# Feed-forward normalisations on ScalarE with factors by GpSimd; scale and bias of the last feed-forward's second norm on VectorE

## The chip, the cores and the metric

The kernel runs on one core of a Trainium2 chip. The time of a run is the device time of that core in microseconds (us), from start to end of the whole program. A separate execution of the same program was recorded by the hardware profiler; its start and end times of single instructions are what "the trace" means below. The engines of a core run side by side, each with its own queue of instructions that it takes in order: TensorE (PE, with its weight loads PEld), VectorE (DVE), ScalarE (ACT), GpSimd (POOL) and SyncE (SP, which only issues DMA transfers here).

## The reference

Four images of 128 channels and 64 x 64 positions pass through two layers. Everything is float32.

- Layer 0, per image: a group norm, then attention over the 4096 positions, with scores from two 64-channel projections, a softmax, and a weighted sum of a 128-channel projection; the result is added to x.
- Layer 1 takes the positions as tokens t of 128 features, `t = t + attention_block(layer_norm(t))`. The attention block has 16 heads of 8 features over blocks of 1024 tokens, whose queries, keys and values are products of cosines. With `w_comb` its context becomes `attn_out`, and then

```python
x1 = _ln(x + attn_out, g1, beta1)
zf = jnp.cos(x1[..., :NQ_FFN]) * jnp.cos(ry_theta)      # 8 of 128 features
h = jax.nn.relu(zf @ w1.T + b1)                          # 512 wide
ffn_out = h @ w2.T + b2
return _ln(x1 + ffn_out, g2, beta2)
```

- Then `t = t + recurrence(layer_norm(t))`: a product with W, a norm over all tokens of all images, and a recurrence with a sigmoid along the tokens.

So each token of the feed-forward passes three normalisations over its 128 features: v, of the context plus its input (times g1, plus beta1); u, of the feed-forward's sum (times g2, plus beta2); and w, of t2, the sum with the token itself, which feeds the recurrence.

## The kernel before

**Stages.** Images are worked on one after the other. For image n, `first_stage` does layer 0 ("the convolution attention"), and `second_stage` does the attention of layer 1. The feed-forward of image n is not a stage of its own for n = 0, 1, 2: it runs inside `first_stage` of image n+1, in the gaps of its attention. The feed-forward of image 3 has no such host, so it runs alone in `third_stage` ("the last feed-forward", `final=True`). Fold of the norm and the recurrence follow. The stages, as the profile's clock has them: convolution attention of image 0 alone at about 63 to 429 us; of images 1, 2 and 3, each with the feed-forward of the image before, at about 1717 to 2219, 3509 to 4009 and 5297 to 5798 us; the last feed-forward at about 7040 to 7192 us.

**The host.** The convolution attention takes rounds over two 128-token blocks of keys and 512 queries: score matmuls into a pair of PSUM banks (`s`, L391; two such pairs exist), one exp over 128 x 1024 on ScalarE (`p`, L399), a running sum of the exps on VectorE (L407), and four matmuls that weigh the values (L414). After each round `meanwhile` is called. It lets the image's own preparation for layer 1 (`tokens`, with transposes, the norm of t, and its cosines) make a step, and then the feed-forward of the image before. Transposes on TensorE all stand at L277, and have `px`, `sum`, `pt`, `pq` as targets for tokens, and `pc`, `pz`, `pt`, `pl` for feed-forward.

**One feed-forward** handles 512 tokens as four blocks of 128; eight make an image. It is a Python generator, and each `yield` ends a step. Two are active at a time in images 0 to 2, and a new one begins at most every 14 steps; in the last feed-forward all eight are active. It loads x1 and adds the bias of `w_comb` (GpSimd, L992), transposes the context (`pc`; copy `cT` on ScalarE, L995), multiplies (`pw`, L1000), adds (v, VectorE, L1002), takes statistics of v; two steps later v is normalised, and GpSimd multiplies by g1 (L1008) and adds the biases (L1009). Then the cosines of 8 features on VectorE (`z` L1017, steps at L237 to L244) with a Sin on ScalarE (L246), a copy that repeats them (`zs`, L1026), transposes (`pz`, `zT` on ScalarE, L1034), the wide layer (`ph` L1043, `hT` on ScalarE L1046) and the narrow one (`pf`, L1054). VectorE adds u (L1064) and takes its statistics; two steps later u is normalised, GpSimd multiplies by g2 (L1069) and adds be2 (L1070); two steps later VectorE adds t2 (L1075) and takes its statistics; two steps later t2 is transposed (`pt`), copied on ScalarE (t2T, L1081) and stored, and w is normalised; two steps later it is transposed (`pl`), copied on ScalarE (L1154), and multiplied with W (`pwx`, L1095).

**Statistics and norms.** `token_stats` does, for each of four blocks, BATCH_NORM_STATS2 (L253) and BATCH_NORM_AGGREGATE (L254) on VectorE; `rsqrt` adds epsilon on VectorE (L230, `v_v`, `v_u`, `v_w`) and raises to -1/2 on GpSimd (L232, `r_v`, `r_u`, `r_w`, 128x4). In images 0 to 2 the norm is `normalise`: four VectorE operations (x - mean) * rstd of 128x128 (L259). In the last feed-forward it is `normalise_act`: VectorE makes `less` = -mean * rstd (L266, 128x4), and four ScalarE activations compute rstd * x + less (L269).

**What sets the order.** In `first_stage` and `second_stage` the orders of TensorE, ScalarE and VectorE are the order in which the program emits instructions; GpSimd's and SyncE's are chosen by the planner of the framework. In the last feed-forward the planner orders all engines.

Of the kernel before, what the change touches and what calls it, by code (L numbers as in the profile page):

```python
# [13 lines left out]
ALU = mybir.AluOpType  # L14
# [12 lines left out]
def kernel(  # L27
# [31 lines left out]
    nc = tc.nc  # L59
# [13 lines left out]
    TG = 4  # L73
# [36 lines left out]
    def get(kind, name):  # L110
        if callable(here[kind]):
            return here[kind](name)
        pool, shape = here[kind]
        return pool.tile(shape, F32, tag=kind, name=name)
# [7 lines left out]
    def half_tile(name):  # L122
        return get("half", name)
# [4 lines left out]
    def one_psum(name):  # L128
        return get("ps_one", name)
# [13 lines left out]
    def load_row(ap, name):  # L143
        return load(ap.partition_broadcast(P), name, (P, ap.shape[-1]))
# [54 lines left out]
    g2_bc, be2_bc = load_row(g2, "g2_bc"), load_row(be2, "be2_bc")  # L199
# [27 lines left out]
    def rsqrt(var, eps, shape, name, pool=small):  # L227

        v = pool.tile(shape, F32, tag=f"var{shape[-1]}", name=f"v_{name}")
        nc.vector.tensor_scalar(v, var, eps, None, ALU.add)  # L230
        r = pool.tile(shape, F32, tag=f"rstd{shape[-1]}", name=f"r_{name}")
        nc.gpsimd.tensor_tensor(r, v, minus_half[: shape[0], : shape[1]], ALU.pow)  # L232
        return r
# [14 lines left out]
    def token_stats(src, n_tiles, eps, name):  # L248

        st = stats.tile([P, n_tiles, 6], F32, tag=f"st{n_tiles}", name=f"st_{name}")  # L250
        mv = stats.tile([P, n_tiles, 2], F32, tag=f"mv{n_tiles}", name=f"mv_{name}")
        for k in range(n_tiles):
            nc.vector.bn_stats(st[:, k, :], src[:, k, :])  # L253
            nc.vector.bn_aggr(mv[:, k, :], st[:, k, :])  # L254
        return mv, rsqrt(mv[:, :, 1], eps, [P, n_tiles], name, stats)

    def normalise(dst, src, mv, rstd, n_tiles):
        for k in range(n_tiles):
            nc.vector.tensor_scalar(  # L259
                dst[:, k, :], src[:, k, :], mv[:, k, 0:1], rstd[:, k : k + 1], ALU.subtract, ALU.mult  # L260
            )

    def normalise_act(dst, src, mv, rstd, n_tiles, name):

        less = stats.tile([P, n_tiles], F32, tag=f"less{n_tiles}", name=f"less_{name}")
        nc.vector.scalar_tensor_tensor(less, mv[:, :, 0], -1.0, rstd, ALU.mult, ALU.mult)  # L266
        for k in range(n_tiles):
            at = slice(k, k + 1)
            nc.scalar.activation(  # L269
                dst[:, k, :], src[:, k, :], AF.Identity, bias=less[:, at], scale=rstd[:, at]  # L270
            )

    def transposed(src, name, kind="ps_one"):

        pt = get(kind, name)
        for k in range(TG):
            nc.tensor.transpose(pt[:, ts(k, P)], src[:, k, :], ident)  # L277
        return pt

    def blocks(ap):  # L280
        return ap.rearrange("p (k e) -> p k e", e=P)

    def row4(bc):
        return bc.unsqueeze(1).broadcast_to([P, TG, P])
# [694 lines left out]
    def feed_forward(im, i, t2_rows, last, final):  # L979


        n, cols = im["n"], ts(i, IC)

        def norm(dst, src, mv, rstd, name):
            if final:
                normalise_act(blocks(dst), blocks(src), mv, rstd, TG, f"{name}{n}_{i}")
            else:
                normalise(blocks(dst), blocks(src), mv, rstd, TG)

        x1 = get("x1", f"fx1_{n}_{i}")  # L990
        nc.sync.dma_start(out=x1, in_=im["x1"][:, cols])
        nc.gpsimd.tensor_tensor(blocks(x1), blocks(x1), row4(bc_bc), ALU.add)  # L992
        pt = transposed(blocks(im["q"][:, cols]), f"pc{n}_{i}")
        cT = get("fhalf", f"cT{n}_{i}")
        nc.scalar.copy(cT, pt)  # L995
        yield

        pa = one_psum(f"pw{n}_{i}")
        for k in range(TG):
            nc.tensor.matmul(pa[:, ts(k, P)], cT[:, ts(k, P)], wc_sb, start=True, stop=True)  # L1000
        v = get("fhalf", f"v{n}_{i}")
        nc.vector.tensor_tensor(v, pa, x1, ALU.add)  # L1002
        yield
        mv, rstd = token_stats(blocks(v), TG, 1e-5, f"v{n}_{i}")
        yield
        yield
        norm(v, v, mv, rstd, "v")
        nc.gpsimd.tensor_tensor(blocks(v), blocks(v), row4(g1_bc), ALU.mult)  # L1008
        nc.gpsimd.tensor_tensor(blocks(x1), blocks(v), row4(fb2_bc), ALU.add)  # L1009
        yield  # L1010
        yield

        z, zk, zr = (
            small.tile([P, TG, D], F32, tag=name, name=f"{name}{n}_{i}") for name in ("z", "zk", "zr")
        )
        be1_z = be1_bc[:, 0:D].unsqueeze(1).broadcast_to([P, TG, D])
        nc.vector.tensor_tensor(z, blocks(v)[:, :, 0:D], be1_z, ALU.add)  # L1017
        steps = cos_steps(zr, z, zk, zr)
        for _ in range(3):
            next(steps)  # L1020
        yield
        yield
        next(steps, None)
        yield
        zs = get("fhalf", f"zs{n}_{i}")
        nc.vector.tensor_copy(  # L1026
            zs.rearrange("p (k r d) -> p k r d", k=TG, d=D),
            zr.unsqueeze(2).broadcast_to([P, TG, P // D, D]),
        )
        yield  # L1030
        yield
        pz = transposed(blocks(zs), f"pz{n}_{i}")
        zT = get("fhalf", f"zT{n}_{i}")
        nc.scalar.copy(zT, pz)  # L1034
        yield
        yield
        hs = []
        for f0 in range(0, NF, 2):
            phs = [one_psum(f"ph{n}_{i}_{f}") for f in range(f0, f0 + 2)]
            hs.append(get("hT", f"hT{n}_{i}_{f0}"))  # L1040
            for j in range(2):
                rows = ds(32 * (f0 + j), D)
                nc.tensor.matmul(phs[j], f1_sb[rows, :], zT[rows, :], start=True, stop=True)  # L1043
            for j in range(2):
                bias = fb1_sb[:, f0 + j : f0 + j + 1]
                nc.scalar.activation(hs[-1][:, j, :], phs[j], AF.Relu, bias=bias)  # L1046
            yield
        yield
        x0 = get("fhalf", f"fx0_{n}_{i}")
        nc.sync.dma_start(out=x0, in_=im["x0"][:, cols])  # L1050
        po = one_psum(f"pf{n}_{i}")
        for k in range(TG):
            for f in range(NF):
                nc.tensor.matmul(  # L1054
                    po[:, ts(k, P)],
                    hs[f // 2][:, f % 2, ts(k, P)],
                    f2_sb[:, f, :],
                    start=f == 0,
                    stop=f == NF - 1,
                )  # L1060
        yield

        u = im["q"][:, cols]
        nc.vector.tensor_tensor(u, po, x1, ALU.add)  # L1064
        mv, rstd = token_stats(blocks(u), TG, 1e-5, f"u{n}_{i}")
        yield
        yield
        norm(u, u, mv, rstd, "u")
        nc.gpsimd.tensor_tensor(blocks(u), blocks(u), row4(g2_bc), ALU.mult)  # L1069
        nc.gpsimd.tensor_tensor(blocks(u), blocks(u), row4(be2_bc), ALU.add)  # L1070
        yield
        yield

        t2 = get("fhalf", f"t2_{n}_{i}")
        nc.vector.tensor_tensor(t2, u, x0, ALU.add)  # L1075
        mv, rstd = token_stats(blocks(t2), TG, 1e-5, f"w{n}_{i}")
        yield
        yield
        pt = transposed(blocks(t2), f"pt2_{n}_{i}")
        t2T = get("fhalf", f"t2T{n}_{i}")  # L1080
        nc.scalar.copy(t2T, pt)  # L1081
        nc.sync.dma_start(out=t2_rows[:, cols], in_=t2T)
        norm(u, t2, mv, rstd, "w")
        yield
        yield
        pt = transposed(blocks(u), f"pl{n}_{i}")
        tokens_i = last(n, i, pt)
        yield
        if n != "r":
            token_products(n, i, tokens_i)  # L1090

    def token_products(n, i, tokens):

        pw = one_psum(f"pwx{n}_{i}")
        nc.tensor.matmul(pw, WT_sb, tokens, start=True, stop=True)  # L1095
        nc.vector.bn_stats(wx_stats[:, n * NIC + i, :], pw)
# [255 lines left out]
    with stage("runs", t2=((P, 2 * IC), 4 * N), half=(HALF, 2 * NS + 2), ps_one=(ONE, 2 * NS)):  # L1352
# [7 lines left out]
        for k in range(2 * NS):  # L1360
            w = half_tile(f"warm{k}")[:, 0 : NN * (C + 1)].rearrange("p (n c) -> p n c", n=NN)
# [28 lines left out]
        with tc.manual_schedule(engines={nc.tensor.engine, nc.scalar.engine}):  # L1390
# [3 lines left out]
            for t in range(-WARM, L):  # L1394
                for k in range(NS):
# [7 lines left out]
                    w = warm[2 * k + t % 2]  # L1403
# [28 lines left out]
        for n, i, t2 in t2s:  # L1432
            eng = nc.sync if i % 2 == 0 else nc.scalar
# [111 lines left out]
```

## Time and profile before

| | us |
|---|---|
| median of 3 runs | 7297.42 (7296.62 to 7308.61) |
| profiled execution, its own time | 7301.42 |
| span of the profiled execution | 7299.6 |
| TensorE busy | 7004.1 (96%) |
| VectorE busy | 6003.5 (82%) |
| ScalarE busy | 5911.8 (81%) |
| GpSimd busy | 2794.4 (38%) |
| convolution attention of image 0, no feed-forward in it | 366 |
| of images 1, 2, 3, with feed-forward | 502, 500, 501 |

The granted TensorE clock was 0.981 over the span. In the lines below, "x" stands ahead of a count. A group's line has the source line, the engine, the operation, output and inputs by the program's names, their partitions x elements, the count, then busy time in us and mean ns of one; after the second bar stands the idle time of the engine just ahead of these instructions, and what ended most of it. A line of waits has the engine and the instruction that waited, what it waited for, then us in total, times, and the longest. A line of a timeline has start and duration in us, and in brackets the idle time before it. `(+1 forms)` means that a group has several shapes. In names, the numbers of image and feed-forward are left out; in the last two norms `q` is the tile that u lives in, `t` is t2 and `fx` is x1 or x0.

### The profile page before, as it was taken

Reading aid. Unit: us, or ns where it says so; the run is one execution under the profiler, and the core shown is the slowest. Engines: PE = TensorE matmul, PEld = TensorE weight load, DVE = VectorE, ACT = ScalarE, POOL = GpSimd, SP = SyncE. Lnnn points to the kernel's source line nnn. Section 1 sums busy time; section 2 is a strip of 40 time slices with the busy share of each in tenths; the row PEclk is TensorE's granted clock in tenths of the full one; section 3 lists DMA queues with packets and bytes.
Section 4 is the critical chain, followed back from the end, with each engine's and each line's share of the span. In section 5 each row is a group of like instructions: output and inputs, shape, how many; then the busy total and the mean of one; then the engine's idle time right before and its main releaser. Section 6 shows DMA issues by size and latency. Waiting matters only on the chain. (4 is left out here: it accounts for less than half of the span.)

```text
span 7299.6 us, 224978 instructions
## 1 busy us (share of the span) xinstructions
PE 7004.1 (96%) x93198; PEld 3502.2 (48%) x93198; DVE 6003.5 (82%) x8097; ACT 5911.8 (81%) x11648; POOL 2794.4 (38%) x9837
## 2 busy tenths in 40 slices
PE   8999999999899999999989999999999899999977
PEld 3445555554444555554444455555444355555546
DVE  5678899887778999889676999889877788888974
ACT  4479999995448999999444999999844599999976
POOL 0034444434223454444422354444522344444542
PEclk9999999999999999999999999999999999999988
DMA  0010000000111000000011100000001110000012
GB/s 28 32 35 24 30 20 21 21 23 13 39 41 37 27 21 20 21 23 20 21 34 45 37 21 20 21 26 19 16 26 37 38 37 21 21 26 27 11 59 105
DMA packets 83101, 212.81 MB, mean 29 GB/s; under 512 B 9120, under 2 KB 10432, under 8 KB 81296
## 3 DMA queue, kind: packets, MB, share of 16 engines
q1 hardware_dynamic: 77312, 186.68, 7.5%
q8 instruction: 733, 12.01, 0.7%
q10 hardware_dynamic: 4304, 11.43, 0.4%
q14 instruction: 304, 2.49, 0.1%
q0 software_dynamic: 448, 0.20, 0.0%
HBM read 141.65 MB, written 56.62 MB: 27 GB/s over the span
## 5 line engine op out<-in xcount | busy, mean ns | idle before, releaser
L886 ACT ACTIVATE e<-s 128x1024 f32<-128x1024 f32 (+1 forms) x3480 | 2949.0, 890 | 61.4 <-PE s L874 38.1
L693 DVE STREAM_TRANSPOSE t<-e 128x1024 f32<-128x1024 f32 x2240 | 2586.9, 1208 | 6.3 <-ACT e L886 3.9
L706 PEld LDWEIGHTS misc<-t,mirror 128*32 128x32 f32 x57344 | 1663.1, 110 | 1410.1 <-issue 1347.8
L706 PE MATMUL misc<-t,mirror 128*32 128x128 f32 x57344 | 1995.2, 273 | 27.6 <-DVE later L720 20.9
L886 ACT ACTIVATE xs<-s 128x1024 f32<-128x1024 f32 (+1 forms) x2152 | 1836.6, 894 | 32.9 <-PE s L874 20.2
L693 DVE STREAM_TRANSPOSE t<-xs 128x1024 f32<-128x1024 f32 x1344 | 1558.4, 1208 | 2.2 <-ACT xs L886 0.7
L727 PE MATMUL acc<-e,q_aug 128*32 128x512 f32 x11360 | 1520.9, 607 | 0.0
L874 PE MATMUL s<-queries,keys 32*128 32x512 f32 x9216 | 1217.2, 495 | 3.9 <-ACT e L886 2.9
L769 POOL COPY own<-o 32x36 f32<-32x36 f32 x2048 | 439.2, 214 | 1708.8 <-DVE o L761 1628.5
L399 ACT ACTIVATE p<-s 128x1024 f32<-128x1024 f32 x512 | 497.7, 1022 | 614.6 <-PE s L391 613.9
L414 PE MATMUL acc<-p,asmT 128*128 128x512 f32 x2048 | 979.4, 611 | 0.0
L727 PE MATMUL acc<-xs,q_aug 128*32 128x512 f32 x7072 | 942.2, 605 | 0.0
L407 DVE TENSOR_TENSOR total<-total,p 128x1024 f32<-128x1024 f32 x448 | 567.9, 1268 | 366.5 <-ACT p L399 343.6
L874 PEld LDWEIGHTS s<-queries,keys 32*128 32x128 f32 x9216 | 480.9, 182 | 491.3 <-issue 373.4
L663 POOL COPY mirror<-q 32x128 f32<-32x128 f32 x2048 | 612.6, 299 | 237.8 <-PE misc L706 150.1
L794 POOL COPY other<-turned 32x64 f32<-32x64 f32 x1904 | 450.9, 237 | 628.0 <-DVE turned L784 549.4
L886 ACT ACTIVATION_READ_ACCUMULATOR e<-s 128x1 f32 x2880 | 651.9, 226 | 0.0
L414 PEld LDWEIGHTS acc<-p,asmT 128*128 128x128 f32 x2048 | 363.0, 192 | 524.2 <-issue 519.7
L391 PE MATMUL s<-e,e 64*128 64x512 f32 x2048 | 533.4, 640 | 7.4 <-DVE asmT L305 7.1
L720 DVE TENSOR_TENSOR later<-later,misc 128x128 f32<-128x128 f32 (+1 forms) x576 | 162.7, 282 | 370.8 <-PE misc L706 366.9
L754 POOL COPY by_token<-by_key 32x4 f32<-32x4 f32 x2016 | 380.8, 189 | 85.2
L727 PEld LDWEIGHTS acc<-e,q_aug 128*32 128x32 f32 x11360 | 225.8, 108 | 348.0 <-issue 330.3
(244 smaller groups left out, 4740.1 us busy)
## 6 DMA issues: line engine op xcount, KB each, us to landing
keys<-parts_dram SPq DMA_DIRECT2D x256, 256.0 KB
queries<-parts_dram SPq DMA_DIRECT2D x1024, 32.0 KB
fx<-x_dram SPq DMA_DIRECT2D x64, 256.0 KB
x_dram<-x SPq DMA_DIRECT2D x56, 256.0 KB
xs<-in_x_dram SPq DMA_DIRECT2D x16, 512.0 KB
t_dram<-t2T SPq DMA_DIRECT2D x32, 256.0 KB
t2s<-t_dram SPq DMA_DIRECT2D x16, 512.0 KB
parts_dram<-high SPq DMA_DIRECT2D x28, 256.0 KB
```

Source lines behind the costliest of these rows:

```text
L391: nc.tensor.matmul(s[:, j, :], e2[rows, ts(2 * jp + j, P)], e1[rows, ts(ic, IC)], start=True, stop=True,)
L399: nc.scalar.activation(p, s, AF.Exp)
L407: nc.vector.tensor_tensor(state[ic], state[ic], p, ALU.add)
L414: nc.tensor.matmul(state["acc", ic], asmT[:, ts(2 * jp + j, P)], p[:, j, :], start=jp == 0 and j == 0, stop=jp == NP - 1 and j == 1,)
L663: nc.gpsimd.tensor_copy(wv[ts(a, 32), s, :, :, ts(a, D)], own[ts(s, 32)])
L693: nc.vector.transpose(group["e"][h][:, k, :], es[h])
L706: nc.tensor.matmul(state["acc"][ts(2 * x + h, 32), :], state["w"][:, QT * (s // 4) + TG * x + s % 4, h, :], state["e"][h][:, :, ds(IC * x ...
L727: nc.tensor.matmul(it["in"]["acc"][ts(2 * h + x, 32), :], it["qa"][:, ds((2 * it["tiles"][x] + h) * V, 32)], it["e"][h][:, ts(x, IC)], sta ...
L769: nc.gpsimd.tensor_copy(own[ts(s, 32), ts(x, 4), h, :], ov[ts(2 * h + x, 32), s, :, 0:V])
L794: copy(to[ts(k, 32), h], tv[ts(2 * x + h, 32), k])
L874: nc.tensor.matmul(ss[h][:, x, :], keys[unit[x] // QT].bitcast(F32R)[r, ts(unit[x] % QT, P)], queries[b].bitcast(F32R)[r, :], start=True, ...
L886: nc.scalar.activation(es[h][:, ts(x, IC)] if split else es[h], ss[h][:, x, :] if split else ss[h].rearrange("p x c -> p (x c)"), AF.Exp, ...
```

## The change

The two factors of each norm are now made together: `norm_factors` takes the statistics, and right after the power GpSimd makes `less` with two operations of its own on 128x4 (a multiplication with the mean, then one with -1), where VectorE made it in one, in the last feed-forward alone, at the time of the norm. All norms v, u and w are ScalarE activations, in every image, at the place in the program where the norm stood. In the last feed-forward g2 and be2 are applied by VectorE; in the other images this stays on GpSimd. The norms of `tokens` are still those of VectorE.

```diff
--- before.py
+++ after.py
@@ -260,10 +260,15 @@
                 dst[:, k, :], src[:, k, :], mv[:, k, 0:1], rstd[:, k : k + 1], ALU.subtract, ALU.mult
             )
 
-    def normalise_act(dst, src, mv, rstd, n_tiles, name):
+    def minus_mean(mv, rstd, n_tiles, name):
 
         less = stats.tile([P, n_tiles], F32, tag=f"less{n_tiles}", name=f"less_{name}")
-        nc.vector.scalar_tensor_tensor(less, mv[:, :, 0], -1.0, rstd, ALU.mult, ALU.mult)
+        nc.gpsimd.tensor_tensor(less, mv[:, :, 0], rstd, ALU.mult)
+        nc.gpsimd.tensor_scalar(less, less, -1.0, None, ALU.mult)
+        return less
+
+    def normalise_act(dst, src, less, rstd, n_tiles):
+
         for k in range(n_tiles):
             at = slice(k, k + 1)
             nc.scalar.activation(
@@ -981,11 +986,12 @@
 
         n, cols = im["n"], ts(i, IC)
 
-        def norm(dst, src, mv, rstd, name):
-            if final:
-                normalise_act(blocks(dst), blocks(src), mv, rstd, TG, f"{name}{n}_{i}")
-            else:
-                normalise(blocks(dst), blocks(src), mv, rstd, TG)
+        def norm_factors(src, name):
+            mv, rstd = token_stats(blocks(src), TG, 1e-5, f"{name}{n}_{i}")
+            return minus_mean(mv, rstd, TG, f"{name}{n}_{i}"), rstd
+
+        def norm(dst, src, factors):
+            normalise_act(blocks(dst), blocks(src), *factors, TG)
 
         x1 = get("x1", f"fx1_{n}_{i}")
         nc.sync.dma_start(out=x1, in_=im["x1"][:, cols])
@@ -1001,10 +1007,10 @@
         v = get("fhalf", f"v{n}_{i}")
         nc.vector.tensor_tensor(v, pa, x1, ALU.add)
         yield
-        mv, rstd = token_stats(blocks(v), TG, 1e-5, f"v{n}_{i}")
-        yield
-        yield
-        norm(v, v, mv, rstd, "v")
+        factors = norm_factors(v, "v")
+        yield
+        yield
+        norm(v, v, factors)
         nc.gpsimd.tensor_tensor(blocks(v), blocks(v), row4(g1_bc), ALU.mult)
         nc.gpsimd.tensor_tensor(blocks(x1), blocks(v), row4(fb2_bc), ALU.add)
         yield
@@ -1062,25 +1068,27 @@
 
         u = im["q"][:, cols]
         nc.vector.tensor_tensor(u, po, x1, ALU.add)
-        mv, rstd = token_stats(blocks(u), TG, 1e-5, f"u{n}_{i}")
-        yield
-        yield
-        norm(u, u, mv, rstd, "u")
-        nc.gpsimd.tensor_tensor(blocks(u), blocks(u), row4(g2_bc), ALU.mult)
-        nc.gpsimd.tensor_tensor(blocks(u), blocks(u), row4(be2_bc), ALU.add)
+        factors = norm_factors(u, "u")
+        yield
+        yield
+        norm(u, u, factors)
+
+        eng = nc.vector if final else nc.gpsimd
+        eng.tensor_tensor(blocks(u), blocks(u), row4(g2_bc), ALU.mult)
+        eng.tensor_tensor(blocks(u), blocks(u), row4(be2_bc), ALU.add)
         yield
         yield
 
         t2 = get("fhalf", f"t2_{n}_{i}")
         nc.vector.tensor_tensor(t2, u, x0, ALU.add)
-        mv, rstd = token_stats(blocks(t2), TG, 1e-5, f"w{n}_{i}")
+        factors = norm_factors(t2, "w")
         yield
         yield
         pt = transposed(blocks(t2), f"pt2_{n}_{i}")
         t2T = get("fhalf", f"t2T{n}_{i}")
         nc.scalar.copy(t2T, pt)
         nc.sync.dma_start(out=t2_rows[:, cols], in_=t2T)
-        norm(u, t2, mv, rstd, "w")
+        norm(u, t2, factors)
         yield
         yield
         pt = transposed(blocks(u), f"pl{n}_{i}")
```

## The prediction

> **What bounds the kernel now.** I read the page's busy table first, then the 40 slices, then a table by stage, then TensorE's waits in one stage, then the groups of instructions of that stage.
>
> ```profile
> PE 7004.1 (96%) x93198; PEld 3502.2 (48%) x93198; DVE 6003.5 (82%) x8097; ACT 5911.8 (81%) x11648; POOL 2794.4 (38%) x9837
> ```
>
> TensorE is the bound over the whole span, so the change can only gain where TensorE stands idle. The table by stage (start and end, length, busy time of PE, PEld, DVE, ACT, POOL, granted clock, DMA share, GB/s) shows where: the convolution attention of image 0 without feed-forward, those of images 1 to 3 with the feed-forward of the image before, and 60 us of the last feed-forward.
>
> ```profile
> 63.00:429.00 366.00, 362.53 (x1220) 145.20 (x1220) 222.97 (x357) 156.54 (x168) 33.43 (x72) 1.00 0.08 27
> 1717.00:2219.00 502.00, 459.89 (x1747) 208.80 (x1745) 358.09 (x770) 220.26 (x257) 137.09 (x146) 0.96 0.11 35
> 3509.00:4009.00 500.00, 458.74 (x1750) 208.79 (x1749) 356.87 (x770) 220.83 (x259) 137.09 (x146) 0.96 0.11 35
> 5297.00:5798.00 501.00, 459.05 (x1751) 209.10 (x1749) 357.67 (x770) 220.53 (x258) 137.12 (x146) 0.96 0.11 35
> 7060.00:7120.00 60.00, 36.22 (x188) 27.40 (x192) 39.96 (x154) 32.97 (x77) 33.73 (x32) 0.64 0.38 140
> ```
>
> With feed-forward TensorE is idle about 42 us per stage, against 3.5 without, and its clock falls from 1.00 to 0.96. What it waits for in the first such stage (us in total, times, longest):
>
> ```profile
> PE pt L277 <- DVE t L1075: 22.7, 5, 7.8
> PE pc L277 <- ACT hT L1046: 5.4, 7, 0.8
> PE pl L277 <- DVE q L259: 4.7, 2, 3.4
> PE pq L277 <- DVE z L1017: 2.8, 1, 2.8
> PE pq L277 <- DVE q L546: 1.9, 1, 1.9
> PE px L277 <- DVE low L562: 1.4, 1, 1.4
> ```
>
> VectorE ends 33.5 of the 42 us (22.7 + 4.7 + 2.8 + 1.9 + 1.4). It is no lack of throughput (358 of 502 us busy) but its written order: several FF and token steps stand behind one another. The groups of that stage (busy, mean ns, idle before and what ended it):
>
> ```profile
> L399 ACT ACTIVATE p<-s 128x1024 f32<-128x1024 f32 x125 | 121.6, 1022 | 142.6 <-PE s L391 142.4
> ...
> L259 DVE TENSOR_SCALAR q<-q,mv_u,r_u 128x128 f32<-128x128 f32 x32 | 17.6, 612 | 0.0
> ...
> L232 POOL TENSOR_TENSOR r_w<-v_w,minus_half 128x4 f32<-128x4 f32 x8 | 13.1, 1643 | 38.1 <-DVE v_w L230 38.1
> ...
> L259 DVE TENSOR_SCALAR v<-v,mv_v,r_v 128x128 f32<-128x128 f32 x32 | 12.0, 438 | 0.7 <-POOL r_v L232 0.7
> ...
> L259 DVE TENSOR_SCALAR q<-t,mv_w,r_w 128x128 f32<-128x128 f32 x32 | 8.9, 340 | 1.2 <-POOL r_w L232 1.2
> ...
> L1075 DVE TENSOR_TENSOR t<-q,fx 128x512 f32<-128x512 f32 x8 | 5.7, 716 | 0.0
> ```
>
> The t2 addition (L1075) never waits for its input: VectorE itself is late. ScalarE waits 142.6 us for scores, so it has room.
>
> **What the Trainium skill says.** "SBUF — State Buffer", section "Who interferes with whom": only the port pair of VectorE and GpSimd contends, as an exclusive lock for a whole instruction; ScalarE has its own ports. The trace agrees: where they start together, L1008 took 2.12 us and L407 2.10, against 1.27 and 1.22 apart, and the same 128x128 norm takes 340 ns for w and 612 for u. "TensorE: Matmul & The Clock Gate", "HAM oscillation": a wait can halve the clock for what follows. The trace agrees: after gaps of 2.8 us and more L414 takes 1.06 us instead of 0.59 for 3 to 4 us, so such a gap costs some 1.5 us more than itself.
>
> **The change, images 0 to 2.** *Off VectorE:* 288 norm instructions: 96 x 611 + 96 x 438 + 96 x 340 ns = 58.7 + 42.0 + 32.6 = 133 us by group means, 115 us as their busy time without overlaps; 38.5 us per stage. *On ScalarE:* 288 activations. Nearest row: the last FF's L269, 485 ns alone and 1.65 us for four in a row (the skill, "ScalarE: Activation LUTs", section "What ACT_TABLE_LOAD costs", gives 280 + 0.833 N ns, an estimate of 387 ns for N = 128): 72 x 1.65 = 119 to 140 us, some 40 to 47 per stage on top of 221 of 500. No table load is added. *On GpSimd:* two 128x4 operations per norm, 144 here. Nearest rows 206 and 220 ns (128x8 and 128x16 additions): 64 us for all at 220 if nothing blocks, at most 1.28 us more each when VectorE holds the pair for an L407. I take 0.5 us per norm.
>
> What that is worth is read gap by gap. In the widest one (7.79 us, from 1874.9) VectorE did norm v 1868.72 to 1870.78 though its factor was ready at 1858.5, then two L407, a cosine step and norm u at 1876.43, though its factor was ready at 1868.5; then L1069 and L1070 on GpSimd to 1880.7, then t2 at 1881.7. Without 2.06 + 1.11 us of norms all of it moves forward 3.2. Likewise, with the norms placed into ScalarE's order at the times of the trace: pq 2.80 saves all; pt 3.85 all; pl 3.45 saves 1.0 (the w norm is then on ScalarE, which takes 1.65 us instead of 1.1); pl 1.3; px 1.0; pt 5.27 saves 2.9; pt 5.57 2.2; pq 1.89 1.5. Sum 19.8. Two gaps vanish that cost slow clock: 3.0 more, 22.8.
>
> What it costs: the new activations stand ahead of exps. In the same placement the next exp is late by 3.45 (v0), 5.68 (u6), 1.2 to 3.0 us (nine others) and about 0 elsewhere. From an exp's end to the scores that reuse its PSUM pair the trace has 3.3 to 9 us, 3.6 to 7.3 where the w norms stand: covered, except u6, 2.3 us. Not covered if the factors come late: after t2T (L1081) ScalarE's next instruction is norm w, which waits for r_w (1.64 us) and the two small operations, with exps queued behind it. I allow 3.4 us per stage (0 to 20). Left: 22.8 - 2.3 - 3.4 = 17 per stage, **-51** for three.
>
> **The change, last feed-forward.** *Off VectorE:* 24 L266 (0.16 us each, 0.82 for v, blocked by L1008). *Onto it:* 8 L1069 and 8 L1070, 1.27 and 1.32 us on GpSimd, as 128x512 operations 0.68 us each like L1075. *GpSimd:* 48 small ones added. The second norms run as a loop, on GpSimd's timeline:
>
> ```profile
> 7131.24 1.02 POOL L232 TENSOR_TENSOR r_u<-v_u,minus_half 128x4 f32<-128x4 f32 x1
> 7135.85 1.27 POOL L1069 TENSOR_TENSOR q<-q,g_bc 128x512 f32<-128x512 f32 x1 [3.59 <-ACT q L269]
> 7137.20 1.27 POOL L1070 TENSOR_TENSOR q<-q,be_bc 128x512 f32<-128x512 f32 x1
> 7138.42 1.02 POOL L232 TENSOR_TENSOR r_u<-v_u,minus_half 128x4 f32<-128x4 f32 x1
> ```
>
> The next r_u stands behind L1070, so a turn lasts about 7.0 us: 1.02 + 3.59 + 2.57. In the changed order g2 and be2 of one FF stand on VectorE ahead of the next one's u (L1064) for about six of eight. A turn becomes: addition, statistics and v_u 2.14, r_u with its wake-up 1.27, factors 0.45, ScalarE's norm between hT 3.27 (down to 1.65), two VectorE operations 1.38: 8.5. Six turns cost 1.5 each, +9; the last FF is no longer gated that way, and the v phase loses L266's wait: -2 and -1 with the tail. I take **+8** (-4 to +14). The GpSimd relief is worth nothing by itself, as it waited 3.59 us for ScalarE in each turn.
>
> Sum: -51 + 8 = -43. Against the profiled execution (7301.4, span 7299.6) this is 7258; against the median of the runs, 7297.4, it is **7254**.
>
> **Rivals.** *Full recovery* (12%): all 33.5 us go, and slow clock with them (9 us in six gaps): -42 x 3 + 8 = -118, with small stalls 7180 to 7205. For it: L1075 waits for nothing. Against: half of each wide gap is GpSimd's L1069/L1070 and the L407s, which stay. *The gaps only move* (16%): t2 still hangs on GpSimd, whose L1069 now waits for ScalarE instead of VectorE, and the last FF takes back the rest: within 15 us, 7285 to 7310. *ScalarE's queue blocks* (20%, slower): a norm at the head of ScalarE's queue waits for factors behind r_w while GpSimd is locked out by L407. Eleven places have on average 2.5 us of cover left beyond my placement; at an extra delay d they cost 11 x (d - 2.5) us per stage, which eats 17 + 8/3 at d of about 4.3. Three GpSimd instructions, each behind one L407, add 3 x 1.28 = 3.8, so it is near. With d = 5 it is -17 x 3 + 27.5 x 3 + 8 = +40; with gaps kept short, 7315 to 7337. Against: mean delays of r_u and r_v (1.3 and 1.0 us) show that most instructions don't meet a lock. That the change does nothing is excluded, since the orders differ.
>
> **How the numbers follow.** The likeliest case (52%) is 7254, by itself 7232 to 7280. 7205 cuts off half of full recovery, 7318 the upper half of the blocking queue: 7205 to 7318 holds about 8 in 10. 0.2%, about what a measurement tells from no change, is 15 us. Faster: 50 + 12 + 5 = 67%; same 14%; slower 19%.
>
> **What would show it.** Right: TensorE idle of about 25 us instead of 42 in each stage with FF, the stages 16 to 18 us shorter, clock above 0.96, waits on t L1075 down to some 12 us, none on norms by VectorE; in the last FF turns of 8 to 9 us between r_u. Wrong: score matmuls (L391) waiting for exps (L399) by several us, L399 waiting for SBUF factors, or idle time ended by GpSimd's small operations far above 0.5 us per norm. If the z or L1017 chain now waits for L1008 behind ScalarE, the gap at pq grows instead of going. The attention stages should not move at all; if they do, my account is incomplete.

## The result, and the profile after

The changed kernel takes 7291.95 us (median of 20 runs, 7283.55 to 7296.19) against 7301.95 for the kernel before, run beside it on the same chip: a ratio of 0.9986, with a 95% interval of 0.998 to 0.9991. That is 10 us: faster, as forecast, and inside the wide range of the prediction, but a quarter of the 43 us forecast, and less than the 0.2% named there as about what can be told from no change. The likeliest case was wrong in size.

The profiled execution has a span of 7291.6 us against 7299.6. Its busy table:

```profile
PE 7007.6 (96%) x93198; PEld 3504.5 (48%) x93198; DVE 5907.3 (81%) x7801; ACT 6015.6 (83%) x11936; POOL 2806.8 (38%) x10013
```

VectorE lost 96 us of work and ScalarE gained 104, as planned. The table by stage of the changed kernel (start and end, length, busy time of PE, PEld, DVE, ACT, POOL, clock, DMA share, GB/s) has the three convolution attentions with feed-forward in their new places:

```profile
1707.00:2203.00 496.00, 458.37 (x1737) 208.18 (x1736) 327.62 (x677) 256.33 (x351) 155.95 (x220) 0.96 0.11 36
3492.00:3989.00 497.00, 458.12 (x1735) 208.74 (x1733) 326.18 (x677) 256.17 (x351) 156.13 (x219) 0.96 0.11 34
5275.00:5774.00 499.00, 458.08 (x1737) 206.81 (x1736) 327.88 (x678) 256.75 (x352) 157.30 (x227) 0.97 0.11 36
```

The times given for the stages ahead of the prediction lie some 10 us late: in the kernel before, the first score matmuls start at 1706.7, 3498.7 and 5286.6 us. Read over 1707 to 2210, 3499 to 3999 and 5287 to 5788 us, VectorE is busy 360.2, 359.0 and 360.3 us there, ScalarE 221 us in each, and TensorE's clock is 0.96 as well. So some 32 us of VectorE work has left each stage, ScalarE has 35 us more, and the stage is 3 to 7 us shorter. To be exact I use two measures of a stage from here on, both from the starts and ends of its matmuls in the one profiled execution of each kernel: its length, from the first score matmul to the last, and TensorE's idle time in it, the sum of all gaps over 0.05 us between one matmul's end and the next one's start.

| | before | after |
|---|---|---|
| lengths of the three stages | 502.9, 500.2, 501.0 | 495.7, 496.9, 498.3 |
| idle time in them | 44.3, 43.4, 44.4 | 37.6, 38.9, 40.9 |
| last score matmul of the last attention to the last matmul of all (the last feed-forward and the recurrence) | 244.24 | 250.95 |

The stages give 13.2 us, the last feed-forward takes 6.7 back, and 1.6 come from the attentions and the hand-overs between: 8.1 to the last matmul. What TensorE waits for in the first such stage, changed kernel (us in total, times, longest):

```profile
PE pt L282 <- DVE t L1083: 12.5, 3, 5.7
PE pc L282 <- ACT hT L1052: 5.4, 7, 0.8
PE pq L282 <- DVE q L551: 3.5, 2, 1.9
PE s L396 <- ACT p L404: 3.1, 1, 3.1
PE pl L282 <- ACT q L274: 2.8, 1, 2.8
PE pq L282 <- DVE z L1023: 2.5, 1, 2.5
PE s L396 <- DVE asmT L310: 1.8, 1, 1.8
PE sum L496 <- ACT x L487: 1.6, 1, 1.6
```

Lines have moved by five to eight: the exp is L404 (before L399), the sum on VectorE L412 (L407), the t2 addition L1083 (L1075), the norm on ScalarE L274. The waits for t2 fell from 22.7 to 12.5 us, as forecast. But three waits are there that were not: for an exp, for ScalarE's copy ahead of `sum`, and for a second product q (1.7 of the 3.5 us). The wait at pl is an old one: a norm by VectorE ended it after 3.4 us, now one by ScalarE does after 2.8; and the wait for asmT, 1.8 us, is in the kernel before too, ahead of the window shown there. What VectorE and ScalarE wait for shows in the groups of this stage, first of the kernel before (over 1707 to 2210 us), then of the changed one:

```profile
L407 DVE TENSOR_TENSOR total<-total,p 128x1024 f32<-128x1024 f32 x111 | 142.4, 1283 | 88.6 <-ACT p L399 83.2
```

```profile
L412 DVE TENSOR_TENSOR total<-total,p 128x1024 f32<-128x1024 f32 x111 | 143.7, 1294 | 116.4 <-ACT p L404 110.4 <-DVE total L412 0.5
...
L274 ACT ACTIVATE q<-t,less_w,r_w 128x128 f32<-128x128 f32 x32 | 13.2, 482 | 19.2 <-POOL less_w L267 19.2
L274 ACT ACTIVATE q<-q,less_u,r_u 128x128 f32<-128x128 f32 x32 | 13.1, 482 | 17.5 <-POOL less_u L267 17.5
L274 ACT ACTIVATE v<-v,less_v,r_v 128x128 f32<-128x128 f32 x32 | 13.1, 484 | 5.2 <-POOL less_v L267 5.2
```

VectorE waits 27 us longer for exps, most of the 32 us that it no longer computes; ScalarE stands 19.2, 17.5 and 5.2 us ahead of norms w, u and v, until GpSimd has their factors. Neither wait is a loss by itself: it becomes one only where TensorE then stands idle. The experiments ask where that is so.

### The profile page after: what moved, and what is told of

It is laid out like the page before. It is cut to its first block, busy times and chain, and to the rows that moved or that the text cites. A ratio compares the mean times of both kernels' runs of the same rounds, so it can differ in the third digit from the quotient of the medians.

```text
span 7291.6 us, 225134 instructions
## 1 busy us (share of the span) xinstructions
PE 7007.6 (96%) x93198; PEld 3504.5 (48%) x93198; DVE 5907.3 (81%) x7801; ACT 6015.6 (83%) x11936; POOL 2806.8 (38%) x10013
## 5 line engine op out<-in xcount | busy, mean ns | idle before, releaser
L412 DVE TENSOR_TENSOR total<-total,p 128x1024 f32<-128x1024 f32 x448 | 571.5, 1276 | 452.5 <-ACT p L404 429.3
L404 ACT ACTIVATE p<-s 128x1024 f32<-128x1024 f32 x512 | 497.0, 1021 | 510.3 <-PE s L396 509.7
```

Source lines behind the costliest of these rows:

```text
L404: nc.scalar.activation(p, s, AF.Exp)
L412: nc.vector.tensor_tensor(state[ic], state[ic], p, ALU.add)
```

## The experiments

Three theories were set against each other. A, the prediction's: the time of the norms on VectorE stands in the gaps nearly one for one, and ScalarE's part is hidden. B: the gain is there, but a norm at the head of ScalarE's queue, waiting for its factors, holds back exps, and with them TensorE and VectorE's sums. C: the gaps don't hang on norm time; GpSimd's lock and VectorE's other work fill them. The table has the sums over the three stages, each from one profiled execution. Only "after", "last feed-forward alone" and the last row change the last feed-forward. "After" and "images 0 to 2 alone" have the same program in these stages; their idle times differ by up to 2.1 us in one stage, and by less than 0.5 us in the sum.

| run | length of the three stages | TensorE idle in them | median of runs, ratio to before (95%) |
|---|---|---|---|
| before | 1504.1 | 132.1 | |
| after | 1490.9 | 117.4 | 0.9986 (0.998 to 0.9991) |
| images 0 to 2 alone | 1487.1 | 117.9 | 0.9978 (0.9968 to 0.9989) |
| last feed-forward alone | 1503.3 | 132.0 | 1.0011 (1.0004 to 1.0018) |
| a quarter of the norms, VectorE | 1473.9 | 106.1 | 0.9954 (0.9937 to 0.997) |
| idle activations added | 1520.2 | 133.2 | 1.0011 (1.0004 to 1.0018) |
| v alone on ScalarE | 1484.9 | 121.0 | 0.9967 (0.9954 to 0.9979) |
| u alone | 1482.7 | 114.5 | 0.9962 (0.995 to 0.9975) |
| w alone | 1508.5 | 137.3 | 1.0008 (0.9999 to 1.0016) |
| u and w late | 1467.9 | 97.6 | 0.9951 (0.9934 to 0.9967) |
| v and late u, w on VectorE | 1466.9 | 104.7 | 0.9939 (0.9923 to 0.9956) |
| g1 and bias on one block | 1470.7 | 102.1 | 0.9952 (0.9936 to 0.9969) |
| u and w late, and the last feed-forward changed but for g2 and be2 | 1468.0 | 97.6 | 0.9952 (0.9936 to 0.9969) |

**The two parts apart.** First the norms of images 0 to 2 alone:

```diff
-            return minus_mean(mv, rstd, TG, f"{name}{n}_{i}"), rstd
+            if not final:
+                return minus_mean(mv, rstd, TG, f"{name}{n}_{i}"), rstd
+            return mv, rstd, f"{name}{n}_{i}"
...
-        eng = nc.vector if final else nc.gpsimd
+        eng = nc.gpsimd if final else nc.gpsimd
```

`norm`, left out here, takes the old way where it is handed the statistics and not the product.

> The change in images 0 to 2 alone; the last feed-forward stays as before (factor by VectorE, g2 and be2 by GpSimd). The stages should add: the three convolution attentions with feed-forward as in the changed kernel, 495.7, 496.9 and 498.3 us between first and last score matmul (before 502.9, 500.2, 501.0), and from the last attention to the last matmul 244 us as before, so about 7284 to 7285 us of span, 15 under the kernel before. If the two parts influence each other the stages differ from these.

The median is 7283.2 us, 18.0 under the kernel before, and the span 7280.1. The stages take 495.6, 495.8 and 495.6 us, and from the last score matmul to the last matmul it is 243.6. Then the last feed-forward alone, with images 0 to 2 as before:

```diff
-            return minus_mean(mv, rstd, TG, f"{name}{n}_{i}"), rstd
+            if final:
+                return minus_mean(mv, rstd, TG, f"{name}{n}_{i}"), rstd
+            return mv, rstd, f"{name}{n}_{i}"
```

> The change in the last feed-forward alone. My prediction gave +8 us for it; by the two traces from the last attention's end to the last matmul it is 251.0 us against 244.2 before. So the convolution attentions as before (502.9, 500.2, 501.0) and +6 to +7 us: slower by 0.1%. If the loss instead comes from the images before, this run is as the kernel before.

The median is 7309.3 us, 8.1 over the kernel before (0.11%), with 252.6 us from the last score matmul to the last matmul. The two parts add: 18.0 less 8.1 is 9.9, and the whole change gained 10.0. The loss at the end was foreseen (+8); what was not is the small gain of the stages.

**Taking away without a price.** The kernel before, with only one of the four blocks of each norm normalised:

```diff
-                normalise(blocks(dst), blocks(src), mv, rstd, TG)
+                normalise(blocks(dst), blocks(src), mv, rstd, 1)
```

> The kernel before, but in images 0 to 2 VectorE normalises only the first of the four blocks of each norm and leaves the other three out (the output is another one); nothing goes to ScalarE. It shows what taking the norms off VectorE is worth with no price elsewhere. Theory A, that of the prediction (VectorE's norm time stands in the gaps one for one): three quarters of 22.8 us per stage and more for the w norm, 15 to 20 us per stage, -45 to -60 in all. Theory B (the gain is real, ScalarE's queue gives it back): the same here. Theory C (norm time is not what the gaps hang on; VectorE then waits for exps or is locked out by GpSimd instead): no more than -5 per stage, -15 in all.

Idle time fell by 26 us in all, 8.7 per stage, and length by 30, 10 per stage. That is between A and C: leaving out three quarters of the norms at no price on ScalarE is worth about half of A's 15 to 20 per stage.

```profile
PE pt L277 <- DVE t L1075: 17.8, 5, 5.8
...
PE pl L277 <- DVE q L259: 4.2, 1, 4.2
PE pq L277 <- DVE q L546: 1.9, 1, 1.9
```

In these waits of its first stage the five gaps ahead of t2 are still there, the longest 5.8 us where it was 7.8, and the one at pq of 1.9 us has not moved at all, as in the changed kernel (1.9, 1.7 and 1.9 us in the three stages): it did not hang on norm time.

**Adding the price without the gain.** The kernel before, with idle activations behind each norm, on a constant:

```diff
                 normalise(blocks(dst), blocks(src), mv, rstd, TG)
+                for k in range(TG):
+                    nc.scalar.activation(
+                        held["gap"][:, ts(k, P)], ident, AF.Identity,
+                        bias=half_pi[:, 0:1], scale=half_pi[:, 0:1],
+                    )
...
-            nc.gpsimd.memset(get("gap", f"gap{n}")[:, 0:1], 0.0)
+            held["gap"] = get("gap", f"gap{n}")
+            nc.gpsimd.memset(held["gap"][:, 0:1], 0.0)
```

> The kernel before with all its norms on VectorE, and in images 0 to 2 besides four activations of 128x128 on ScalarE at the place of each norm, from one constant to a spare tile: they wait for nothing and nobody waits for them. It shows the price of ScalarE's time alone, without waits for factors. Theory A: hidden in ScalarE's 142 us of waiting per stage, under +3 us per stage. Theory B (time in ScalarE's queue makes exps late, and VectorE's sums and TensorE with them): +5 to +12 us per stage, +15 to +36 in all. Theory C: as A.

Idle time is that of before, 133.2 against 132.1, and the gaps are the same to some 0.5 us each. The activations took 486 ns each and held up next to nothing that TensorE waited for (0.4 us at `sum`). So with VectorE's own norms in place, time on ScalarE alone is hidden, as A said. The stages were 16 us longer all the same, 7.0 and 9.3 in the first and third and nothing in the second, all of it in slower matmuls: length less idle time is 465.5, 456.0 and 465.5 us, against 458.6, 456.8 and 456.6. The clock that the trace records accounts for it: it is 0.94, 0.96 and 0.94 in these stages, against 0.96 in all three before. It stands at full or at half speed, and 47.9, 28.1 and 48.3 us of the matmul time fell into stretches at half, against 34.0, 30.0 and 29.4 before. Take half of that off, and all six stages have 441.4 to 441.9 us left. Why the clock was halved more often in two of three stages stays open; the gaps, which are the same, do not explain it.

**One norm at a time.** The condition of the first diff is narrowed to one name, here v; the other two runs have u and w in its place:

```diff
-            if not final:
+            if not final and name == "v":
```

> In images 0 to 2 only the v norms go to ScalarE with factors by GpSimd; u and w norms and the last feed-forward stay as before. TensorE's idle time in a convolution attention with feed-forward is 44 us before and 39 with all three norms moved. Theory B (the price is the norm standing at the head of ScalarE's queue for its factors): v's factors are made long before (ScalarE waited 6 us per stage for them, against 17 for u and 20 for w), so v alone keeps its gain and pays little: idle 38 to 41 us per stage, without the stalls ahead of sum (3.2 us) and score matmuls (3.2 us) if those are u's and w's. Theory C (what returns the gain is GpSimd's lock, moved onto other VectorE operations): idle 43 to 45, since v's removal also moves L1008 and L1009 into the token norms.

> In images 0 to 2 only the u norms go to ScalarE. Theory B: the stall of 3.15 us of a score matmul is u's (norm u of the seventh feed-forward waits for its factors with two exps behind it), so it shows here; with u's share of the gaps before t2 regained idle is 41 to 44 us per stage. Theory C: 43 to 45 with no stall of score matmuls.

> In images 0 to 2 only the w norms go to ScalarE. Theory B: each stands right behind t2T and waits for r_w and two small operations (20 us per stage), so exps and sums come later: gaps ahead of pl stay about 2.8 us, and idle is as before or worse, 43 to 47 us per stage. Theory C: -1 us per stage, 43.

Idle time changed by -3.7, -5.9 and +1.7 us per stage, in the order v, u, w. So v and u pay, and w costs a little: its run is not slower than the kernel before beyond the noise (1.0008, 0.9999 to 1.0016). The gain of u is larger than either theory expected, though its norm holds up a score matmul by 2.2 us in every stage, as B foresaw. The run of v has such a stall too, of 2.0 us in the first and third stages, which B did not foresee. Together the three changes would be -7.9; all three in one kernel gave -4.8. TensorE's waits in the first stage of w alone show a wait of the kind foreseen, but at another place:

```profile
PE pt L288 <- DVE t L1096: 22.8, 5, 7.8
...
PE sum L502 <- ACT x L493: 3.2, 1, 3.2
```

The waits for t2 are those of before, and `sum` now waits 3.2 us for a copy by ScalarE. The timeline of that run at this place (start, duration, in brackets the idle time before; the first row is VectorE's sum that runs beside the power on GpSimd; rows that do not bear on it are left out):

```profile
1827.08 1.22 DVE L415 TENSOR_TENSOR total<-p,p 128x1024 f32<-128x1024 f32 x1
1827.25 2.02 POOL L232 TENSOR_TENSOR r_w<-v_w,minus_half 128x4 f32<-128x4 f32 x1 [4.79 <-DVE v_w L230]
...
1829.34 0.20 POOL L266 TENSOR_TENSOR less_w<-mv_w,r_w 128x4 f32<-128x4 f32 x1
...
1829.63 0.23 POOL L267 TENSOR_SCALAR less_w<-less_w 128x4 f32<-128x4 f32 x1
...
1829.90 1.65 ACT L274 ACTIVATE q<-t,less_w,r_w 128x128 f32<-128x128 f32 x4 [2.71 <-POOL less_w L267]
...
1831.57 1.28 ACT L410 ACT_TABLE_LOAD   x1
1832.86 1.94 ACT L410 ACTIVATE p<-s 128x1024 f32<-128x1024 f32 x2
...
1834.68 0.59 ACT L493 COPY x<-px 128x512 f32<-128x512 f32 x1
...
1835.33 1.04 PE L502 MATMUL sum<-total,ones 128*32 128x128 f32 x16 [3.22 <-ACT x L493]
```

r_w took 2.02 us and the factors 0.5 more; ScalarE waited 2.7 us with a table load, two exps and the copy of x behind the norm, and the whole row came late to TensorE. My placement had looked at the next exp and its PSUM pair, and not at the copy behind it.

**Curing the wait.** The change in images 0 to 2 alone, with norms u and w one step later, inside the steps that were there, so that t2 and pl keep theirs:

```diff
         factors = norm_factors(u, "u")
         yield
         yield
+        if not final:
+            yield
         norm(u, u, factors)
...
         yield
-        yield
+        if final:
+            yield
...
+        if not final:
+            yield
         norm(u, t2, factors)
         yield
-        yield
+        if final:
+            yield
```

> As the run with the change in images 0 to 2 alone, but there norm u (with g2 and be2 behind it) and norm w are emitted one step later, out of the two steps that follow each, so that t2 and pl keep their steps. The factors are then ready when ScalarE comes to the norm, and an exp goes ahead. Theory B: ScalarE's waits for factors (20 and 17.5 us per stage) fall below 10 and the stalls ahead of sum and score matmuls (6.4 us per stage) go: idle 30 to 35 us per stage, against 39. Against that stands that t2 and pl have a step less: if the chain through GpSimd's g2 and be2 binds, the gaps ahead of t2 grow and idle stays at 39 or rises. Theory C: the same 39 or more.

ScalarE's waits for factors of w and u in the first stage fell to 10.5 and 12.2 us, a little short of the 10 expected. Idle time is 32.0, 32.1 and 33.4 us, 6.8 per stage less than with all three norms at their old steps, and the median, 7266.7 us, is 36 under the kernel before. TensorE's waits in the first stage:

```profile
PE pt L288 <- DVE t L1099: 13.5, 4, 5.7
...
PE pl L288 <- ACT q L274: 2.8, 1, 2.8
PE pq L288 <- DVE q L557: 2.5, 2, 1.9
```

The waits of a score matmul for an exp and of `sum` for the copy are gone, and the gap of 2.5 us at pq by z has shrunk to 0.8: B is shown for these. The step less for g2 and be2 was not free. The waits for t2 are 13.5 us here against 10.9 in the first stage of the run with the change in images 0 to 2 alone, about 2 more per stage over the three, and VectorE now waits for GpSimd's be2 ahead of t2:

```profile
L418 DVE TENSOR_TENSOR total<-total,p 128x1024 f32<-128x1024 f32 x111 | 140.5, 1266 | 106.5 <-ACT p L410 101.2
...
L1099 DVE TENSOR_TENSOR t<-q,fx 128x512 f32<-128x512 f32 x8 | 5.5, 689 | 5.7 <-POOL q L1093 5.7
```

The first of these lines says that VectorE's longer waits for exps are no measure of the loss: they are still 101.2 us, 18 more than before, in a run with 11.5 us less idle time per stage than before.

**Without w.** Norms v and u on ScalarE, u late as in the diff above, w on VectorE as before, and the last feed-forward too:

```diff
-            if not final:
+            if not final and name != "w":
```

> In images 0 to 2 v and u norms on ScalarE, u one step later; w norms on VectorE at their old place; last feed-forward as before. Theory B: w on ScalarE was worth nothing by itself (idle 45.8 us per stage against 44.0), so without it and with u's wait covered this is as good as late u and w or better: idle 29 to 33 us per stage, about 7255 to 7265. If w's VectorE time (8.9 us per stage) counts once the waits are gone, it is worse: idle 34 to 38.

Idle time is 36.2, 33.0 and 35.5 us, 34.9 on average, more than with the late w and in the range where w's VectorE time counts; yet the stages are as short in sum (1466.9 against 1467.9), since their matmuls ran a little faster. At a median of 7259.4 us, 0.61% under the kernel before, this is the fastest kernel here, though its interval overlaps that of the late norms.

**GpSimd's lock.** The first part of the change, with GpSimd's g1 and the bias behind it applied to one block of four in images 0 to 2, the rest left out:

```diff
-        nc.gpsimd.tensor_tensor(blocks(v), blocks(v), row4(g1_bc), ALU.mult)
-        nc.gpsimd.tensor_tensor(blocks(x1), blocks(v), row4(fb2_bc), ALU.add)
+        part = slice(0, TG if final else 1)
+        nc.gpsimd.tensor_tensor(blocks(v)[:, part], blocks(v)[:, part], row4(g1_bc)[:, part], ALU.mult)
+        nc.gpsimd.tensor_tensor(blocks(x1)[:, part], blocks(v)[:, part], row4(fb2_bc)[:, part], ALU.add)
```

> The change in images 0 to 2 alone (last feed-forward as before), but there g1 and the bias behind it (L1008 and L1009 of the kernel before) are applied by GpSimd to the first of four blocks only; the rest is left out. These two are not on the chain to the next t2. In the changed kernel they fall onto the token norms of VectorE, which take 3.2 us instead of 1.1 ahead of the widest gap. If that lock is why this gap shrank from 7.8 to 5.7 us only, and not to the 4.6 of my working, it is 3 to 4.5 us here, the lock going and L407 and z with it. If it is VectorE's order and its waits for exps alone, it stays at 5.5 to 6.

The gap that was widest, 7.8 us before and 5.7 to 6.0 with the change, is 4.0 us in each of the three stages, within 3 to 4.5. Over all gaps this run has 5.3 us less idle time per stage than the change in images 0 to 2 alone (102.1 against 117.9 us in sum), not far from the 6.8 of the late norms, so the lock weighs nearly as much as the place of norms u and w. In the timeline of the changed kernel the token norms ahead of that gap meet these two:

```profile
1864.98 3.22 DVE L259 TENSOR_SCALAR x<-x,mv_t,r_t 128x128 f32<-128x128 f32 x4
...
1864.99 1.27 POOL L1014 TENSOR_TENSOR v<-v,g_bc 128x512 f32<-128x512 f32 x1 [3.87 <-ACT v L274]
1866.34 1.26 POOL L1015 TENSOR_TENSOR fx<-v,fb_bc 128x512 f32<-128x512 f32 x1
```

Before, these four norms took 1.11 us, since L1008 and L1009 came later and met a sum and a cosine step of VectorE instead. With the two cut down they took 1.52. So an earlier v norm moved GpSimd's work onto other VectorE work, and 2.1 us of the 3.2 that norms no longer took went into the lock here. The sum and the cosine step did not get faster for it: in the changed kernel they meet GpSimd's addition of a bias to x1 and its g2, and take 2.30 and 1.75 us, against 2.11 and 1.75 before. It is the exclusive lock that the Trainium skill's "SBUF — State Buffer" tells of under "Who interferes with whom", on which the prediction drew for its prices but not for where the lock would move.

**The last feed-forward.** The changed kernel with both late norms and with g2 and be2 left on GpSimd at the end:

```diff
-        eng = nc.vector if final else nc.gpsimd
+        eng = nc.gpsimd if final else nc.gpsimd
```

> The changed kernel with norms u and w one step later in images 0 to 2, and with g2 and be2 of the last feed-forward left on GpSimd (factors by GpSimd and norms by ScalarE there as in the change). The convolution attentions should repeat those of the run with late norms (idle 32 to 33 us, 486 to 493 us). In the last stage: if, as my prediction says, it is g2 and be2 in VectorE's order that lengthen the turn between one r_u and the next from 7.0 to 8.5 us, it is 244 us or less from the last attention's end to the last matmul, 240 to 244 with L266 off VectorE; if the two small operations on GpSimd are what costs, it stays near 251.

The median is 7267.1 us. The three stages repeat those of the late norms (493.3, 486.7, 487.9), and from the last score matmul to the last matmul it is 244.43 us, against 250.95 in the changed kernel and 244.24 before; runs with that part as before have 243.1 to 244.3. So 6.5 of the 6.7 us are g2 and be2 on VectorE, and the factors on GpSimd gain and lose nothing there on balance. The mechanism stands in the timeline of the changed kernel:

```profile
7117.96 1.40 POOL L232 TENSOR_TENSOR r_u<-v_u,minus_half 128x4 f32<-128x4 f32 x1 [6.90 <-DVE v_u L230]
...
7123.29 0.69 DVE L1077 TENSOR_TENSOR q<-q,g_bc 128x512 f32<-128x512 f32 x1 [4.83 <-ACT q L274]
...
7124.50 0.69 DVE L1078 TENSOR_TENSOR q<-q,be_bc 128x512 f32<-128x512 f32 x1
...
7125.11 0.68 DVE L1070 TENSOR_TENSOR q<-pf,fx 128x512 f32<-128x512 f32 x1
...
7127.50 1.04 POOL L232 TENSOR_TENSOR r_u<-v_u,minus_half 128x4 f32<-128x4 f32 x1 [7.55 <-DVE v_u L230]
```

VectorE waits 4.8 us for ScalarE's norm with the next u (L1070) behind it; the next r_u can't start until that is done. The eight r_u lie 57.4 us apart from first to last, 8.2 per turn (7.6 to 9.5 but for the last one of 6.1), against 48.8 and 7.0 before. With g2 and be2 back on GpSimd they lie 52.3 us apart, so its turns are still 0.5 us longer than before; it makes that good with 1.0 us ahead of the first r_u and 2.3 behind the last.

## Why the prediction was right or wrong, point by point

- *What bounds the kernel:* right in that TensorE gains only in its gaps; the t2 waits fell by 10 us in the first stage, to the 12 forecast. The stages were read over windows 10 us late; that left out one gap of 1.8 us and changes nothing in the argument.
- *The gains, gap by gap, 19.8 us per stage:* here is the step that failed most. The measured gain is about 13.8 (old gaps of before less what is left of each, mean of the three stages). Right were pt 3.85, pl 1.29 and px, which went as said, and pt 5.27 (saved 3.2 or more). Too much was put on pq 2.80 (saved 0.3 of 2.8), pq 1.89 (nothing for 1.5), pt 5.57 (0.8 for 2.2), pt 7.79 (2.0 for 3.2) and pl 3.45 (0.6 for 1.0). The prediction took it that what stands behind the norms in VectorE's order moves forward by their time; at pt 7.79 in the words "without 2.06 + 1.11 us of norms all of it moves forward 3.2". Two things are against it. VectorE's other work ahead of the gap does not keep its durations when GpSimd's L1008 and L1009 move with the norm, shown at pt 7.79 by the run with these cut down. And VectorE's sums do not move forward when the exps they wait for come later. At pq 2.80 the changed kernel has VectorE waiting 3.25 us for an exp that stands behind norms v and u on ScalarE; with u one step later that wait is 1.8 us and the gap 0.8. But the gap is 0.7 to 0.9 us too with g1 and the bias on one block, so those two operations of GpSimd have a part there, and how large a part is not settled. At pt 5.57 too much norm time was read: between VectorE's last wait, which ends at 2128.1, and that t2 its row holds 1.0 us of norm u (2139.11 to 2140.13) and no other of these norms; the quarter run leaves 4.8 us of that gap, the change 4.7. At pq 1.89 no run with fewer norms on VectorE shortened the gap, and what it hangs on stays open.
- *Slow clock, 3.0 us per stage:* wrong. Length less idle time is 458.1, 458.0 and 457.4 us against 458.6, 456.8 and 456.6: 0.5 more per stage, and 33.1, 32.2 and 29.6 us of it at half clock against 34.0, 30.0 and 29.4. Matmul time wandered from 452.7 to 461.3 among runs with fewer gaps, and to 465.5 where gaps were unchanged. Some slow stretches follow a gap, but the number of wide gaps does not set their sum.
- *The price, 2.3 + 3.4 us per stage:* the stall at u6 was right in place and nearly in size (a score matmul, 3.15 us in all three stages). The allowance was too small: with sum (1.6 to 3.2), pq (1.5 to 1.7), pz (0.8 to 1.0) and the rest, new gaps are 9.0 per stage, where 5.7 were put; that is inside the bounds of 0 to 20. One term in it: the two small operations were put at 0.5 us per norm, and in the first stage took 0.4 for v, 0.9 for u and 0.9 for w. (Their sum of 64 us is a slip, 144 times 0.22 is 32; nothing was built on it.) The idle activations and the late norms together show that it is mostly the place of the norm in ScalarE's order that costs, and not ScalarE's time as such. At pq 2.80, though, no factor was late: there the exp stood behind eight activations in a row, and their time itself counted, since VectorE had nothing left to do meanwhile. The idle activations, run beside VectorE's own norms, could not show that.
- *The stages' sum, 17 us:* the three terms fell short by 6.0, 3.5 and 3.3 us; 17.1 less these is 4.3, and the stages measured 4.4 each on average.
- *The last feed-forward, +8:* right in mechanism and near in size, +6.7, with turns of 8.2 us for 8.5. Its own terms, +9, -2 and -1, make +6 and not +8, so that the closeness of the total is in part luck; seven turns measured 8.6 us more, and 1.9 came back outside them.
- *Rivals:* "ScalarE's queue blocks" was a real mechanism at a third of its price at most (9.0 us of new gaps per stage, not all of them ScalarE's, for 27.5), so it did not turn the sign, but it ate most of the 13.8 us gained. The sign named for it, score matmuls waiting for exps by several us, came. "The gaps only move" named the time that came, 7285 to 7310, and in part the reason: the last feed-forward took some back. Its other reason did not hold: t2's addition waits for nothing on GpSimd in the first stage of the changed kernel (0.0 us ahead of L1083); it is still VectorE that is late. That the result lies inside the prediction's range owes much to the range's width.

## What to carry to other kernels

Moving work off an engine whose order sets the gaps pays only if the work behind it can start: look at what its next instructions wait for and whom they will now collide with, before adding durations. On the engine that receives the work, time that waits for nothing may be nearly free, while the same instruction waiting for a factor holds up all that stands behind it, not the next exp alone; one step later in the program cured most of that here (36 us gained against 18). And an operation that moves from a side engine into another engine's order brings its wait along: here two operations of 0.7 us each put a wait of 4.8 us ahead of the next feed-forward's u.

## What was not expected of the hardware

Matmul time in stages with the same work varied without any change in idle time: 456.0 to 465.5 us between stages of one execution (the idle activations), so differences of a few us in a stage's length are not to be laid to an instruction unless the gaps show it. The recorded clock accounts for nearly all of it: less half of what ran at half clock, matmul time is 440.3 to 443.9 us in all three stages of all thirteen kernels, where as measured it is 452.7 to 465.5. The same 128x4 power on GpSimd took 1.0 us for v on average, and 2.02 us for w in the timeline shown, where a sum of VectorE ran beside it.
